# A decoder kernel: the first attention recorded in a fixed order, with the context attention's beginning beside its steps

## The chip, the cores and the metric

The kernel runs on 1 core of one Trainium2 chip. The metric is the device time of one execution in microseconds (us); the time before is 4245.74 us, the median of 3 runs (4244.13 to 4250.96). Five engines run side by side, each through its own queue in order: TensorE (PE) multiplies and transposes, VectorE (DVE) and ScalarE (ACT) work element by element, GpSimd (POOL) does a few additions, and SyncE (SP) issues the loads. An instruction waits on semaphores for the results that it needs, and whatever stands behind it in the same queue waits with it.

## The reference, cut to what matters

Two decoder layers work on `x` of 4 x 1024 x 256 in float32. Each layer has a self attention, a context attention and a feed-forward part. The change touches layer 0 only, up to the first steps of its context attention:

```python
def _L0_attn_ref(x, Wq, bq, Wk, bk, Wv, bv, Wo, bo):          # one head of 128
    Q = jnp.einsum('bsd,hd->bsh', x, Wq) + bq
    K = jnp.einsum('bsd,hd->bsh', x, Wk) + bk
    V = jnp.einsum('bsd,hd->bsh', x, Wv) + bv
    scores = jnp.where(causal, jnp.einsum('bqh,bkh->bqk', Q, K), -jnp.inf)
    attn = jax.nn.softmax(scores * jnp.float32(HEAD_DIM) ** (-0.5), axis=-1)
    return jnp.einsum('bsh,dh->bsd', jnp.einsum('bqk,bkh->bqh', attn, V), Wo) + bo

x = x + _L0_attn_ref(_layernorm(x), ...)
x = x + _L0_xattn_ref(_layernorm(x), ctx_1024, ...)           # 16 heads of 16, 77 context rows per batch
x = x + _L0_ffn_ref(_layernorm(x), ...)                       # ternary weights, 8 bit activations
x = x + _L1_attn_ref(_layernorm(x), ...); x = x + _L1_xattn_ref(...); x = x + _L1_ffn_ref(...)
return x
```

## The kernel before, in words

All of `x` stays in four SBUF tiles `X[b]` (128 rows x 8 tiles x 256), one for each batch; `load_x` issues their eight loads first of all. `B` is 4, `NTB` is 8 row tiles of 128 in a batch, `S` is 1024, `Z` is 77.

`l0_attn` (line 161) goes through the batches. For each it takes the row statistics of the eight tiles on DVE (lines 111 and 112), the root of the variance by a power on POOL (line 70), normalizes on DVE (line 118), adds the output bias to `X[b]` on POOL (`add_row`, line 156), turns the normalized tiles on PE (line 129) and copies the turned blocks alternately on DVE and ACT (`net.copy`, lines 141 and 143). Queries and keys are eight matmul passes of 512 columns each (line 191; a float32 matmul is two passes, so two halves by two parts by two passes), finished on ACT (line 194); the values are 32 passes of 128 columns (line 200), finished on DVE (line 204). Then each row tile `i` of the batch has eight stages:

1. scores on PE (line 214), only the `i + 1` blocks that the causal mask leaves
2. the mask on DVE (line 217), the row maximum `nm` (219) and its scaled copy `nb` (221)
3. the exponential on ACT with the row sum (line 224), and the sum's reciprocal on DVE (225)
4. `i + 1` transposes on PE (line 231)
5. their copies to `prT`, alternately on DVE and ACT (lines 141 and 143)
6. `i + 1` products with the values on PE (line 235)
7. a copy to `aT`, alternately on DVE and ACT
8. the projection on PE (line 240), added to `X[b]` on DVE (line 241).

No order is written out for this function: the framework's scheduler decides where each instruction stands in its engine's queue, and pools decide how far work may run ahead (two PSUM buffers for scores, two for transposes, two for outcomes).

When `l0_attn` has ended, its pools close, `Ffn` makes its tiles, and `l0_xattn` (line 247) begins: its weights are loaded into memory that the first attention has just left; `below`, the context keys `kb` (line 289 on PE, 294 on DVE) and values `v` (303 and 306) are made. From here on the order of PE, DVE and ACT is written out by hand (`manual_schedule`). `prologue(b)` is a generator of eight pieces which normalizes batch `b` again and makes the context attention's queries `qT`; `prologue(0)` runs through first. Then a loop over `u`, half a batch each, and four slots `s` in it: `maxima(u + 1, s)` (PE line 383, DVE 391 and 395; `turned` transposes the result at line 401 and copies it at 402), `weigh` of the slot before, `exponentials(u, s)` (PE lines 418 and 423, ACT 427), `outcome` (lines 447 to 467), and pieces of other work: one piece of `ahead` (the next batch's `prologue`) and three of `behind` (`ffn.weights`, which loads eight parts of the feed-forward weights, line 847, takes their absolute sums, line 858, and quantizes them, lines 812 to 814; later `ffn.rows`). The loop begins at `u = -1`, a round of four slots that has no exponentials yet:

```python
            ahead.append(prologue(0))
            while ahead:
                piece(ahead)
            neg = following = first = second = None
            ...
            for u in range(-1, U):
                if u % 2 and (u + 1) // 2 + 1 < B:
                    ahead.append(prologue((u + 1) // 2 + 1))
```

So `prologue(1)` runs beside the rounds -1 and 0, and the weights beside the rounds -1, 0 and 1. The feed-forward part, layer 1's attention (which takes most of the time, line 1312 above all) and the rest follow in the same order in both kernels.

Of the kernel before, what the change touches and what calls it, by code (L numbers as in the profile page):

```python
# [10 lines left out]
F32 = mybir.dt.float32  # L11
# [8 lines left out]
P = 128  # L20
B, S, D = 4, 1024, 256
Z = 77
NTB = S // P
# [6 lines left out]
class Net:  # L30
# [14 lines left out]
    def load_x(self):  # L45
        x = self.ins["x"].rearrange("(b t p) d -> b p t d", b=B, p=P)
        for b in range(B):
            for h in range(2):
                ts = slice(h * NTB // 2, (h + 1) * NTB // 2)
                self.nc.sync.dma_start(self.X[b][:, ts, :], x[b][:, ts, :])  # L50
# [110 lines left out]
def l0_attn(net):  # L161

    tc, nc = net.tc, net.nc
    with ExitStack() as ctx:
        w = ctx.enter_context(tc.tile_pool(name="w1", bufs=1))
        p2 = ctx.enter_context(tc.tile_pool(name="p1_2", bufs=2))
        p3 = ctx.enter_context(tc.tile_pool(name="p1_3", bufs=3))
        ps_s = ctx.enter_context(tc.tile_pool(name="ps1_s", bufs=2, space=PSUM))
        ps_t = ctx.enter_context(tc.tile_pool(name="ps1_t", bufs=2, space=PSUM))
        ps_o = ctx.enter_context(tc.tile_pool(name="ps1_o", bufs=2, space=PSUM))  # L170
# [3 lines left out]
        wo = net.load(w, "L0_attn_WoT", [P, D])  # L174
        bq = net.load(w, "L0_attn_bq", [P, 1])
        bk = net.load(w, "L0_attn_bk", [P, 1])
        bv = net.load_row(w, "L0_attn_bv", P)
        bo = net.load_row(w, "L0_attn_bo", D)
        causal = net.load(w, "c_causal", [P, P])
        scale = float(np.float32(P) ** np.float32(-0.5))  # L180
        for b in range(B):
            xnT = net.normalized_t(b, p2, ps_t)
            net.add_row(b, bo)
            qT = p2.tile([P, S], F32, name="qT")
            kT = p2.tile([P, S], F32, name="kT")
            for wt, bias, dst in ((wq, bq, qT), (wk, bk, kT)):
                for n in range(2):
                    cols = bass.ts(n, 512)
                    po = ps_o.tile([P, 512], F32, name="po")
                    for c in range(2):  # L190
                        nc.tensor.matmul(
                            po, wt[:, c, :], xnT[:, c, cols], start=(c == 0), stop=(c == 1)
                        )
                    nc.scalar.activation(dst[:, cols], po, AF.Identity, bias=bias)
            v = p2.tile([P, NTB, P], F32, name="v")
            for g in range(2):
                po = ps_o.tile([P, 4, P], F32, name="po")
                for t in range(4):
                    for c in range(2):
                        nc.tensor.matmul(  # L200
                            po[:, t, :], xnT[:, c, bass.ts(4 * g + t, P)], wv[:, c, :],
# [3 lines left out]
                    v[:, 4 * g : 4 * g + 4, :], po, bv.unsqueeze(1).to_broadcast([P, 4, P]), ALU.add  # L205
                )
            aT = p2.tile([P, S], F32, name="aT")
            rinv = p2.tile([P, NTB], F32, name="rinv")
            for i in range(NTB):
                n = (i + 1) * P  # L210
                sc = ps_s.tile([P, S], F32, name="sc")
                for j in range(0, n, 512):
                    m = min(512, n - j)
                    nc.tensor.matmul(
                        sc[:, j : j + m], qT[:, bass.ts(i, P)], kT[:, j : j + m], start=True, stop=True
                    )
                nc.vector.tensor_tensor(sc[:, n - P : n], sc[:, n - P : n], causal, ALU.add)
                nm = p3.tile([P, 1], F32, name="nm")
                nc.vector.tensor_reduce(nm, sc[:, :n], AX.X, ALU.max, negate=True)
                nb = p3.tile([P, 1], F32, name="nb")  # L220
                nc.vector.tensor_scalar(nb, nm, scale, None, ALU.mult)
                pr = p3.tile([P, S], F32, name="pr")
                sm = p3.tile([P, 1], F32, name="sm")
                nc.scalar.activation(pr[:, :n], sc[:, :n], AF.Exp, bias=nb, scale=scale, accum_out=sm)
                nc.vector.reciprocal(rinv[:, i : i + 1], sm)
# [2384 lines left out]
```

## Time and profile before

| what | value |
|---|---|
| median of 3 runs | 4245.74 us (4244.13 to 4250.96) |
| the profiled execution: its own time, its span | 4258.2 us, 4256.2 us |
| busy over the whole span | PE 93%, DVE 70%, ACT 38%, POOL 24% |
| granted PE clock, mean | 0.971 |
| first product on PE | at 10.8 us |
| last addition of the first attention (line 241) | at 191.4 us |
| first product of the context attention (line 289) | at 202.3 us |
| round -1 of the context attention's loop | 220.6 to 240.4 us |
| round 0 | 240.4 to 276.0 us |
| last exponentials of round 7 (line 427) | begin at 495.7 us |

In an answer by stretches, each line has the stretch, its length, then the busy time of PE, of PE's weight loads (PEld), DVE, ACT and POOL with the number of instructions, the granted PE clock (1.00 is full speed), the share of the DMA engines and the GB/s. In a timeline, each line has start, duration, engine, line of the code, operation, output<-input, and in brackets the idle time of the engine just before and what ended it. The profiled execution took 12.5 us more than the median, so a difference worked out in it is carried over to the median as it stands.

### The profile page before, as it was taken

Reading aid. Unit: us, or ns where it says so; the run is one execution under the profiler, and the core shown is the slowest. Engines: PE = TensorE matmul, PEld = TensorE weight load, DVE = VectorE, ACT = ScalarE, POOL = GpSimd, SP = SyncE. Lnnn points to the kernel's source line nnn. Section 1 sums busy time; section 2 is a strip of 40 time slices with the busy share of each in tenths; the row PEclk is TensorE's granted clock in tenths of the full one; section 3 lists DMA queues with packets and bytes.
Section 4 is the critical chain, followed back from the end, with each engine's and each line's share of the span. In section 5 each row is a group of like instructions: output and inputs, shape, how many; then the busy total and the mean of one; then the engine's idle time right before and its main releaser. Section 6 shows DMA issues by size and latency. Waiting matters only on the chain.

```text
span 4256.2 us, 58168 instructions
## 1 busy us (share of the span) xinstructions
PE 3957.2 (93%) x22392; PEld 2840.0 (67%) x22392; DVE 2992.6 (70%) x5484; ACT 1605.6 (38%) x2557; POOL 1026.4 (24%) x1218
## 2 busy tenths in 40 slices
PE   7889758999999999999999999997889899899999
PEld 5544324888788887888878877784555555557765
DVE  6555687889778987789878888776667567543224
ACT  2234445344333343333433333332555454212220
POOL 2000000334333433333333333331000000012215
PEclk9989979999999999999999999998999999899999
DMA  1010000000000000000000000000000000301213
GB/s 48 25 35 1 1 22 2 1 1 1 1 1 1 1 1 1 1 1 1 1 1 1 1 1 1 1 1 27 1 1 1 1 1 11 113 23 61 64 42 108
DMA packets 50911, 64.37 MB, mean 15 GB/s; under 512 B 8557, under 2 KB 44769, under 8 KB 50625
## 3 DMA queue, kind: packets, MB, share of 16 engines
q1 hardware_dynamic: 44145, 42.81, 3.2%
q0 software_dynamic: 6480, 17.70, 1.5%
q8 instruction: 185, 3.03, 0.3%
q14 instruction: 101, 0.83, 0.1%
HBM read 42.80 MB, written 17.69 MB: 14 GB/s over the span
## 4 chain that ended last, share of the span: by engine, by line
PE 67%; DVE 15%; ACT 2%; issue 1%; another core or an unknown queue 0%; DMA 0%; DVEq 0%; ACTq 0%; SPq 0%
PE sc L1312 35%; PE po L1341 5%; PE ph L2364 4%; PE ph L2292 3%; PE sc L1800 3%; DVE nm L1813 3%; DVE mx L1320 2%; DVE pr L1330 2%; PE po L1882 2%; PE po L2394 2%; PE po L2279 2%; PE pt L1748 1%; DVE prT L1851 1%; DVE km L1302 1%; PE pt L1850 1%
## 5 line engine op out<-in xcount | busy, mean ns | idle before, releaser
L1312 PE MATMUL sc<-qT,km 128*128 128x256 f32 x8064 | 1794.7, 382 | 9.0 <-DVE pr L1330 9.0
L1312 PEld LDWEIGHTS sc<-qT,km 128*128 128x128 f32 x8064 | 1521.8, 190 | 275.1 <-issue 62.4
L1333 ACT ACTIVATE pr<-pr,zb 128x1024 f32<-128x1024 f32 x512 | 588.2, 1149 | 1327.9 <-DVE pr L1330 1308.0
L1322 POOL PARTITION_ALL_REDUCE top<-mx x512 | 545.8, 1066 | 1466.1 <-DVE mx L1320 1466.1
L1320 DVE TENSOR_REDUCE mx<-sc 128x256 f32<-128x1024 f32 x512 | 625.2, 1221 | 323.1 <-PE sc L1312 321.6
L1330 DVE TENSOR_TENSOR pr<-sc,top 128x1024 f32<-128x1024 f32 x512 | 621.0, 1213 | 0.0
L1302 DVE SCALAR_TENSOR_TENSOR km<-kT,w_L_attn_conv_w,km 128x512 f32<-128x512 f32 x504 | 380.5, 758 | 24.7 <-ACT km L1289 20.0
L1325 POOL COPY tops<-top 32x256 f32<-32x256 f32 x512 | 269.6, 526 | 32.5
L1341 PE MATMUL po<-pr,v 128*32 128x256 f32 x4096 | 249.2, 384 | 0.0
L1813 DVE TENSOR_REDUCE nm<-sc 128x1 f32<-128x1024 f32 x128 | 156.1, 1220 | 79.4 <-PE sc L1800 79.3
L1827 ACT ACTIVATE pr<-sc,nb,rq 128x1024 f32<-128x1024 f32 x128 | 155.1, 1212 | 129.3 <-PE pt L1857 110.1
L1341 PEld LDWEIGHTS po<-pr,v 128*32 128x32 f32 x4096 | 120.4, 110 | 109.6 <-issue 43.2
L2364 PE MATMUL ph<-wgu,xnT 128*128 x568 | 180.4, 460 | 2.2 <-issue 1.6
L1289 ACT ACTIVATE km<-kT,w_L_attn_conv_w 128x512 f32<-128x512 f32 x252 | 173.5, 707 | 5.3 <-PE po L1095 5.3
L1850 PE MATMUL pt<-ident,pr 128*128 128x128 f32 x1024 | 142.7, 280 | 21.9 <-DVE X L1901 12.3
L2371 DVE TENSOR_TENSOR xnT<-ph,xnT 128x352 f32<-128x352 f32 x71 | 37.2, 524 | 171.0 <-ACT xnT L2370 133.8
L1865 POOL COPY rb<-rinv 128x256 f32<-128x256 f32 x32 | 12.9, 402 | 592.0 <-DVE rinv L1841 314.6
L1850 PEld LDWEIGHTS pt<-ident,pr 128*128 128x128 f32 x1024 | 111.4, 142 | 47.0 <-issue 18.8
L2364 PEld LDWEIGHTS ph<-wgu,xnT 128*128 128x128 f32 x568 | 102.3, 190 | 49.0 <-issue 3.0
L1800 PE MATMUL sc<-kT,qT 64*128 64x512 f32 x512 | 133.1, 624 | 0.2 <-ACT pr L1827 0.2
L1882 PE MATMUL po<-prT,v 128*64 128x256 f32 x1024 | 133.1, 392 | 0.2 <-DVE oT L1889 0.2
L1851 ACT COPY prT<-pt 128x512 f32<-128x512 f32 x128 | 68.9, 589 | 142.5 <-PE pt L1850 142.5
(515 smaller groups left out, 4871.7 us busy)
## 6 DMA issues: line engine op xcount, KB each, us to landing
yrows<-xnT SPq DMA_DIRECT2D x71, 128.0 KB, 1.7
X<-in_x SPq DMA_DIRECT2D x8, 512.0 KB, 8.0
out<-X SPq DMA_DIRECT2D x8, 512.0 KB, 2.8
wgu<-in_L_ffn_w_gate SPq DMA_DIRECT2D x8, 352.0 KB, 6.7
wgu<-in_L_ffn_w_up SPq DMA_DIRECT2D x8, 352.0 KB
raw<-in_L_ffn_w1T SPq DMA_DIRECT2D x4, 512.0 KB
raw<-in_L_ffn_w2T SPq DMA_DIRECT2D x4, 512.0 KB, 3.7
xrows<-xn SPq DMA_DIRECT2D x2, 1024.0 KB
```

The lines of the kernel that those rows point to most:

```text
L1302: nc.vector.scalar_tensor_tensor(km, keys, weight, km, ALU.mult, ALU.add)
L1312: nc.tensor.matmul(sc[:, j, :], km[:, c, bass.ts(j, P)], qT[:, c, bass.ts(i, Q2)], start=(c == 0), stop=(c == 1),)
L1320: nc.vector.tensor_reduce(mx, sc.rearrange("p j q -> p q j"), AX.X, ALU.max)
L1322: nc.gpsimd.partition_all_reduce(top, mx, P, bass_isa.ReduceOp.max)
L1325: nc.gpsimd.tensor_copy(tops[n][rows, i % (NQ, 2)[n], :], top[rows])
L1330: nc.vector.tensor_tensor(pr, sc, top.unsqueeze(1).to_broadcast([P, KT, Q2]), ALU.subtract)
L1333: nc.scalar.activation(pr, pr, AF.Exp, bias=zb[:, h : h + 1])
L1341: nc.tensor.matmul(po[32 * e : 32 * e + 32, :], v[:, n * KT + j, 4 * g + e, :], prs[e][:, j, :], start=(j == 0), stop=(j == KT - 1),)
L1800: nc.tensor.matmul(sc[e][:, bass.ts(n, 512)], lhsT[at], kT[at, d, bass.ts(n, 512)], start=True, stop=True,)
L1813: nc.vector.tensor_reduce(nm, sc[e], AX.X, ALU.max, negate=True)
L1850: nc.tensor.transpose(pt[:, n, :], pr[e][:, bass.ts(j + n, P)], net.ident)
L2364: nc.tensor.matmul(ph[:, k, :F], s["xT"][:, c, :], wgu[:, bass.ds(s["e"] * GU + (2 * c + k) * F, F)], start=(c == 0), stop=(c == 1),)
```

## The change

- `l0_attn` becomes a generator that shares the context attention's PSUM pools, and its order on PE, DVE and ACT is written out by hand. One step handles one row tile, 32 steps in all. A step records, in this order: the scores of its tile, the transposes (and copies) of the tile two steps behind, the mask and maximum of its own, the projection of the tile four steps behind, planned work, the exponential of its own, work handed in by the context attention (`beside`), and the products with the values of the tile two steps behind.
- The planned work of batch b + 1 stands in the eight steps of batch b: normalizing in the steps 0 to 3, and turning, queries, keys and values in the steps 4 to 7, three units each. The statistics of batch b + 2 stand in the steps 4 to 7 (`measure`). Batch 1 is an exception: its statistics stand in steps 1 to 3 and all of its normalizing in step 3. Batch 0 prepares its first half ahead of step 0, and the rest in steps 0 to 3.
- Normalizing goes from DVE to ACT (half of batch 0's stays). The power on POOL becomes twelve small DVE operations and one for the offset. All copies of turned tiles go to ACT; of the turned probabilities, the first four blocks go to DVE and the others to ACT; the copy to `aT` goes to ACT. The values are finished in pairs of tiles, and the bias is added on POOL in halves (1024 instead of 2048 columns).
- Row tiles go from the largest to the smallest in batches 1 to 3, and in the order 0, 1, 2, 3, 7, 6, 5, 4 in batch 0.
- The context attention's weights are loaded into memory of their own, behind the first attention's weights and the other batches of `x`. `context_keys` stands in steps 8 and 9, `context_values` in 10 to 13, `prologue(0)` and `prologue(1)` piece by piece in steps 16 to 30, and the four `maxima(0, k)` in steps 32 to 35, where only the tail of the first attention is left. Round -1 goes, and the loop begins at `u = 0`. `Ffn`'s tiles and the pool of its weights (`p2`) are made only when the first attention has ended, so the pieces of `ffn.weights` stand beside the rounds 0, 1 and 2.
- After that, the order of the instructions is that of the kernel before. The number of matmuls is the same.

```diff
-def l0_attn(net):
+def l0_attn(net, ps_s, ps_t, beside):
...
+        net.load_x(range(1, B))
+        yield
...
-        for b in range(B):
-            xnT = net.normalized_t(b, p2, ps_t)
-            net.add_row(b, bo)
...
+            def of(self, first, n):                       # class Statistics
+                for t in range(first, first + n):
+                    nc.vector.bn_stats(self.st[:, t, :], net.X[self.b][:, t, :])
+                    nc.vector.bn_aggr(self.mv[:, t, :], self.st[:, t, :])
+
+            def root(self, first, n):
+                ts = slice(first, first + n)
+                nc.vector.tensor_scalar(self.var[:, ts], self.mv[:, ts, 1], LN_EPS, None, ALU.add)
+                r = net.rsqrt(p2, self.var[:, ts], P, n, f"x{first}_{n}")
+                nc.vector.scalar_tensor_tensor(
+                    self.off[:, ts], self.mv[:, ts, 0], -1.0, r, ALU.mult, ALU.mult
+                )
...
+            def normal(self, st, first, n, shared=False):  # class Batch
+                for t in range(first, first + n):
+                    x, r = net.X[self.b][:, t, :], st.r[t]
+                    if shared and t % 2:
+                        nc.vector.tensor_scalar(
+                            self.xn[:, t, :], x, st.mv[:, t, 0:1], r, ALU.subtract, ALU.mult
+                        )
+                    else:
+                        nc.scalar.activation(
+                            self.xn[:, t, :], x, AF.Identity, bias=st.off[:, t : t + 1], scale=r
+                        )
+
+            def biased(self, h):
+                x = net.X[self.b][:, h * HT : (h + 1) * HT, :]
+                nc.gpsimd.tensor_tensor(
+                    x, x, bo.unsqueeze(1).to_broadcast([P, HT, D]), ALU.add
+                )
...
+        def prepare(bt, st, step):
+
+            if bt.b == 1:
+                measure(st, [step + k for k in range(1, 4)])
+                for h in range(2):
+                    plan(step + 3, lambda h=h: bt.normal(st, h * HT, HT), lambda h=h: bt.biased(h))
+            else:
+                for k in range(4):
+                    plan(step + k, lambda k=k: bt.normal(st, 2 * k, 2))
+                    if k % 2:
+                        plan(step + k, lambda k=k: bt.biased(k // 2))
+            for k, do in enumerate((
+                (bt.turn, 0), (bt.turn, 1), (bt.turn, 2),
+                (bt.turn, 3), (bt.query, 0), (bt.key, 0),
+                (bt.query, 1), (bt.key, 1), (bt.value, 0),
+                (bt.value, 1), (bt.value, 2), (bt.value, 3),
+            )):
+                plan(step + 4 + k // 3, lambda do=do: do[0](do[1]))
...
+        while True:
+            b, k = divmod(step, NTB)
+            if b < B:
+                if k == 0:
+                    now = bt
+                    if b < B - 1:
+                        bt = Batch(b + 1)
+                        prepare(bt, stats.pop(b + 1), step)
+                    if b < B - 2:
+                        stats[b + 2] = Statistics(b + 2)
+                        measure(stats[b + 2], [step + k for k in range(4, 8)])
+                i = (k if k < HT else 3 * HT - 1 - k) if b == 0 else NTB - 1 - k
+                tiles.append(Tile(now, i))
+                tiles[step].scores()
+            if 2 <= step < B * NTB + 2:
+                tiles[step - 2].turned()
+            if b < B:
+                tiles[step].maxima()
+            if 4 <= step < B * NTB + 4:
+                tiles[step - 4].project()
+            for do in at.pop(step, []):
+                do()
+            if b < B:
+                tiles[step].exponentials()
+            more = beside(step)
+            if 2 <= step < B * NTB + 2:
+                tiles[step - 2].weigh()
...
-            ahead.append(prologue(0))
+            ahead += [prologue(0), prologue(1)]
+            for c in range(2):
+                with_step(NTB + c, context_keys, c)
+            for b in range(B):
+                with_step(NTB + 2 + b, context_values, b)
+            for k in range(16):
+                with_step(2 * NTB + k, piece, ahead)
+            for k in range(4):
+                with_step(B * NTB + k, lambda k: turns.append(maxima(0, k, following)), k)
+                with_step(B * NTB + 1 + k, lambda: turns.pop(0)())
+            for _ in before:
+                pass
             while ahead:
                 piece(ahead)
+            p2 = ctx.enter_context(tc.tile_pool(name="p2_2", bufs=2))
+            ffn = new_ffn()
+            behind = [ffn.weights(p2, ps_t)]
...
-            for u in range(-1, U):
+            for u in range(U):
```

## The prediction

> **What bounds the kernel now.** I read the slices of the page first. PE is the fullest engine, but not at the beginning, and its clock drops there too:
>
> ```profile
> PE   7889758999999999999999999997889899899999
> PEclk9989979999999999999999999998999999899999
> ```
>
> A slice is 106 us, so the change plays in the first two and a half. I cut these into stretches (columns as in the section before):
>
> ```profile
> 0.00:10.81 10.81, 0.00 (x1) 0.00 (x1) 5.17 (x25) 1.28 (x1) 2.38 (x7) 1.00 0.85 283
> 10.81:26.50 15.69, 14.91 (x63) 10.03 (x64) 13.97 (x37) 3.92 (x6) 6.37 (x3) 1.00 0.39 123
> 26.50:38.50 12.00, 1.00 (x8) 0.60 (x6) 12.00 (x44) 0.50 (x3) 8.41 (x3) 0.68 0.00 0
> 38.50:66.90 28.40, 26.36 (x142) 19.26 (x143) 17.87 (x44) 9.10 (x23) 3.66 (x2) 0.90 0.01 1
> 66.90:108.20 41.30, 37.95 (x217) 27.43 (x216) 22.91 (x62) 13.79 (x32) 4.51 (x1) 1.00 0.00 1
> ...
> 191.40:202.25 10.85, 0.00 (x0) 0.00 (x1) 7.95 (x35) 0.00 (x0) 2.10 (x3) 0.64 0.56 171
> 202.25:220.60 18.35, 17.57 (x56) 10.12 (x56) 6.76 (x15) 3.12 (x5) 4.52 (x1) 0.84 0.15 41
> 220.60:240.40 19.80, 7.40 (x73) 5.15 (x72) 17.32 (x47) 1.75 (x5) 0.00 (x0) 0.62 0.17 54
> ```
>
> Three holes stand out: 12 us in which the scheduler let DVE do later batches' normalizing first, 10.9 us until the context attention's weights have landed, and round -1, where DVE is full and PE waits. The waits name them:
>
> ```profile
> ACT pr L224 <- DVE nb L221: 47.6, 20, 14.0
> PEld pt L231 <- ACT pr L224: 24.3, 15, 11.4
> PE pt L401 <- DVE tops L395: 12.4, 4, 3.9
> PE pt L289 <- DMA w_c_sel<-in_c_sel: 10.9, 1, 10.9
> ```
>
> **The work of PE that is left.** In the timeline eight passes of 512 columns begin 3.43 us apart from the next group: 0.43 each; 32 passes of 128 take 3.46, 0.107 each; 256 columns then take 0.215. A batch has 180 passes of 128 for scores, transposes and products (72 + 36 + 72: 19.3 us), 32 for values (3.4), 16 turns (1.7), 16 passes of 512 (6.9), 16 of 256 for the projection (3.4): 34.7 us, where the kernel takes 41.3 to 41.8. Four batches: 139. Context keys and values (8 passes of 308, 16 of 256): 5.5. Two prologues of 16 turns and 16 passes of 512: 17.2. Four `maxima` of 0.93: 3.7. Together 165.4 us up to round 0, which now begins at 240.4.
>
> **What PE will wait for, by walking through the steps.** On DVE I use 0.69 us for a copy of 512 columns (0.42 for 256, 0.28 for 128), 0.30 for the mask, 1.22 down to 0.28 for a maximum, 0.14 for `nb`, 0.48 for the projection's addition, 0.15 for a reciprocal, 0.42 for the values of two tiles, 0.53 for the statistics of a tile (the spacing at 192 us), 2.4 for the twelve root operations (196.3 to 198.8) and 0.2 for the offset, 0.36 for a normalized tile; on ACT 0.52 for a normalized tile (2.07 for four).
>
> - Lead-in. The first half of `X[0]` is there at 4.75. Four statistics (2.1) and a root (2.6) end at 9.5, so PE begins at about 10.3, as before. Turns, queries and keys of half a batch run at the slow pace of before's first passes (0.86 for 512), and ACT finishes the keys: scores at 17.3, with 4.3 us of work done. Lost: 13.0.
> - Steps 3 to 5. Batch 1's root ends at about 30.6; eight normalized tiles on ACT stand ahead of step 3's exponential, whose buffer the scores of step 5 want. PE is there at 32.5 and goes on at 36. Lost: 3.5.
> - Products behind the copy of `prT`: in steps without planned PE work only the projection (0.43) covers 0.69 and the handover, 0.3 us in some twelve steps: 3.5.
> - POOL's additions. Beside one of them DVE's normalizing stood still, as these two groups of eight show:
>
> ```profile
> 19.31 6.86 DVE L118 TENSOR_SCALAR xn<-X,mv_x,rstd_x 128x256 f32<-128x256 f32 x8 [1.30 <-POOL rstd_x L70]
> ...
> 70.07 2.67 DVE L118 TENSOR_SCALAR xn<-X,mv_x,rstd_x 128x256 f32<-128x256 f32 x8 [0.28 <-PE pt L129]
> ```
>
>   The difference is 4.2 us for an addition of 4.5. The bias now comes in eight halves of some 2.25 us (estimate, half of 4.5) between `nb`s, and twice whole. Ends: nothing, or 8 x 2.25 + 2 x 4.5 = 27. Most of it falls on DVE's slack; I take 2.
> - Steps 15 to 20, where DVE becomes the bound. Step 15: 1.9 for the tile, 1.3 for values, 1.1 for statistics, 2.6 for the root: 6.9, PE 4.2. Step 16: 2.7 and four statistics (2.1), PE 2.8. Step 17: 2.4 and 2.1, PE 2.3. Step 18: 2.7, a root, two normalized tiles: 5.8, PE 4.3. DVE 22.0 against 13.6, as each product waits for a copy queued behind all that. In 19 and 20 the prologue's turns wait for tiles normalized behind the same queue. The walk gives 33.6 us for 22.6 of PE. Lost: 11.
> - Steps 23 to 31, the same for `prologue(1)`, with little PE work beside it since no batch follows: waits of 0.4, 2.2, 5.8 (step 26, its turn), 2.7 and 2.7. Lost: 14.
> - Steps 32 to the start of round 0: masks and maxima of the context attention (3.6, then three times 1.5 on DVE) in series with PE, some 15 us for 6.2 of PE. Lost: 8.8.
>
> Sum: 165.4 + 13.0 + 3.5 + 3.5 + 2 + 11 + 14 + 8.8 = 221.2. Round 0 begins 19.2 us earlier.
>
> The Trainium skill ("SBUF — State Buffer", Who interferes with whom) says that DVE in a two-port mode and GpSimd exclude each other for whole instructions; every half bias would then cost its full 2.25 wherever DVE is the bound, which is in steps 15 to 19 (two of them) and 28: some 7 instead of 2. It also says ("TensorE: Matmul & The Clock Gate", Part 1) that an idle window of about 3.4 us halves the clock, and a busy one restores it; that speaks against the long wait of step 26 and the tail, and would add about 2 us for each. Neither figure is in the sum.
>
> **What else moves.** Loads: the other three batches of `x` now stand behind nine small loads on SP, which took 7.5 us to issue (7.6 to 15.1). `X[1]` is then issued at 10 and, by the page's 8.0 us to landing, there at 18, when step 1's statistics want it: 0 to 2 us of DVE, nothing in the sum. The context attention's weights follow, long before step 8; `raw` and the two feed-forward rows stay behind the first attention's end. The first sum stands one slot (about 8 us) behind its load, and one that was free took 3.7 to land, so I cost it at nothing; if its memory came free late, DVE would stop there for at most a landing, 4 us. ACT takes 28 normalized tiles (14.6 us), eight turned copies and eight copies to `aT` more, beside the 61 us that it worked in 240; apart from steps 3 to 5 that is hidden. Round 0 loses `prologue(1)`'s 8 us of PE, but its slots are bound by a chain (maxima, DVE, exponentials on PE, ACT 1.93): the four took 9.95, 8.57, 7.89 and 9.17. I keep the first, which ran at a low clock, and give 7.9 to the others: 33.6 for 35.6, gain 2. Three quantizations (2.15 each on DVE) move into round 2, whose DVE was busy 11.1 of 32: cost 1. Total: 19.2 + 2 - 1 = 20.2. The profiled execution would go from 4258.2 to 4238; carried over to the median 4245.7, that is 4225.
>
> **Rivals.**
> 1. The walk is too strict, and PE stays the bound through steps 15 to 31 as the copies are ready early. Then 20 of the 25 us there go, and 5 elsewhere: about 4200. For it: only PE's order and two buffers of scores force the meeting. Against: each product stands behind a copy in DVE's queue.
> 2. Slower: the fixed order ends each step in a handover (product waits for copy, copy behind the last step's maximum and addition). If that costs 1.2 us in each of 32 steps instead of the 3.5 us above, it adds 35: 4260. It decides from 1.0 us a step ((20.2 + 3.5 + 8.5) / 32). For it: before, the last tile, in series, took 8 us from its scores (182.5) to its projection (190.6). Against: two tiles of distance, where DVE has 2.5 to 3 us of 3.5 to 5.
> 3. It does not do what it says: the holes close, but PE's clock falls in the new ones. The rows grant 0.62 to 0.68 around holes. At 0.65 the 62 us of PE work in steps 15 to 20 and 23 to 31 take 33 more; the 25 of waits cover about half of it: 16 more, 4241, no change.
>
> **How the numbers follow.** About 0.2% (8.5 us) is what can be told from no change. My forecast gets 0.75, rival 1 0.10 (both faster), rival 3 0.09 (the same), rival 2 0.06 (slower). Range: down by 15 for the DVE waits and 7 for products and lead-in, up by 5 for POOL, 4 for the load and 8 for the clock: 4203 to 4242, which leaves out half of rivals 1 and 3 and all of 2.
>
> **What would show it.** Right: the 12 us and 10.9 us holes gone, scores from about 17 us, batches of 37 to 40 us, small PE waits on DVE in steps 15 to 20 and 24 to 28 with the root and normalizing in front, first exponentials of round 0 at about 223 us, and later stages shifted as a whole. Wrong: waits of PE on copies in every step; a clock below 0.9 from 60 to 200 us; DVE waiting for `raw` in round 0; or a change behind 300 us.

## The result, and the profile after

The changed kernel takes 4219.28 us (median of 4 runs, 4217.14 to 4222.46), the kernel before in the same comparison 4247.82. The ratio is 0.9937, with a 95% interval from 0.9924 to 0.9950: 28.5 us less. The forecast was 20.2 us less, or 4225.

Lines of the code have moved: L323 scores, L352 transposes, L357 and L359 the copies to `prT` on DVE and ACT, L365 products with the values, L368 the copy to `aT`, L374 projection, L231 normalizing on ACT, L246 turns, L256 queries and keys, L129 and L534 the prologues' turns and queries, L480 context keys, L573 the products of `maxima`, L585 its maximum, L591 its transpose. The profiled execution took 4222.46 us, its span 4220.7. The slices of the page, PE and its clock:

```profile
PE   8899568999999999999999999997989899899999
PEclk9989889999999999999999999998999999899999
```

PE's first slice rises from 7 to 8 and its third from 8 to 9; the fifth and sixth, 7 and 5 before, are 5 and 6, since what follows comes earlier. Behind them one digit of PE differs. The same in stretches (columns as before), cut at the scores of steps 0, 8, 16, 21 and 23, at the end of step 31's products and at round 0:

```profile
19.82:65.67 45.85, 42.43 (x219) 29.86 (x220) 27.19 (x93) 20.14 (x45) 7.01 (x3) 0.93 0.14 33
65.67:109.27 43.60, 43.60 (x262) 33.82 (x261) 28.40 (x89) 19.42 (x46) 4.71 (x2) 1.00 0.00 1
109.27:134.85 25.58, 20.26 (x123) 14.80 (x121) 23.60 (x85) 13.03 (x30) 4.72 (x2) 1.00 0.00 1
...
152.29:197.12 44.83, 40.90 (x227) 29.12 (x226) 29.49 (x95) 15.19 (x39) 4.54 (x1) 1.00 0.00 1
197.12:213.25 16.13, 11.24 (x87) 7.10 (x85) 10.77 (x22) 1.87 (x8) 0.00 (x0) 0.66 0.10 34
213.25:246.89 33.64, 28.12 (x189) 12.62 (x189) 8.27 (x10) 9.34 (x15) 0.00 (x0) 0.81 0.10 32
```

The two holes of 12 and 10.9 us are gone. Subtract the busy time of PE from the length: PE has no idle time in steps 8 to 15, 5.3 us in steps 16 to 20 (where DVE is busy for 23.6 of 25.6), 3.9 in steps 23 to 31, and 4.9 in the tail, where its clock is low too. Round 0 begins at 213.25 instead of 240.40, 27.2 us earlier. The first scores of layer 1's last attention stage (L1800 before, L2008 after) stand at 2956.9 instead of 2986.1, 29.2 earlier; layer 1's first scores (L1312, L1520) came 26.5 earlier (722.0 for 748.5). Round 0 itself took 2.0 less. So the change lies before and in round 0, within a wobble of some 3 us that later stages add between any two of these executions. (The spans differ by 35.5. The other 6 lie in the feed-forward products at the end of layer 1, L2500, which took 577.9 us from first to last in some profiled executions and 582.1 in others, whatever the edit, and 584.0 in that of before.)

The waits of PE up to round 0, each with total, count and longest:

```profile
PE pt L246 <- ACT xn L231: 12.7, 5, 10.3
PE pt L365 <- DVE prT L357: 7.2, 7, 1.7
PE pt L591 <- DVE rinv L369: 2.7, 1, 2.7
PE pt L591 <- DVE tops L585: 2.1, 2, 1.7
PE pt L129 <- DVE xn L118: 1.7, 1, 1.7
```

The first is the lead-in (10.3) and steps 3 to 5; the second is DVE in steps 16 to 18, 24 to 26 and 31; the third and fourth lie in the tail; the last is the wait of step 26, for which the forecast had 5.8. The lead-in and steps 3 to 5 in the timeline of PE:

```profile
12.90 3.78 PE L256 MATMUL pt<-xnT,w_L_attn_WqT 128*128 128x512 f32 x4 [0.68 <-ACT xnT L249]
...
19.82 0.49 PE L323 MATMUL sc<-kT,qT 128*128 128x128 f32 x2 [0.78 <-ACT kT L260]
...
35.76 0.33 PE L246 MATMUL pt<-ident,xn 128*128 128x128 f32 x1 [1.97 <-ACT xn L231]
...
40.02 1.65 PE L365 MATMUL pt<-prT,v 128*128 128x128 f32 x6 [0.96 <-ACT aT L368]
41.47 3.19 PE L323 MATMUL sc<-kT,qT 128*128 128x512 f32 x4
```

Such a group of four passes of 512 columns takes 3.78 and 3.19 us here, and 1.88 where the same line stands at 46.12: PE ran at half clock, in the second case from 38.3 to 45.2. And steps 16 and 17, where each product waits for a copy on DVE, which stands behind statistics and the root in step 16 and behind four statistics in step 17:

```profile
113.38 0.71 PE L365 MATMUL pt<-prT,v 128*128 128x128 f32 x4 [1.57 <-DVE prT L357]
...
117.78 0.49 PE L365 MATMUL pt<-prT,v 128*128 128x128 f32 x2 [1.65 <-DVE prT L357]
```

### The profile page after: what moved, and what is told of

Same layout as the page of the kernel before. It is cut to its first block, busy times and chain, and to the rows that moved or that the text cites. A ratio compares the mean times of both kernels' runs of the same rounds, so it can differ in the third digit from the quotient of the medians.

```text
span 4220.7 us, 58215 instructions
## 1 busy us (share of the span) xinstructions
PE 3950.9 (94%) x22392; PEld 2841.7 (67%) x22392; DVE 2984.2 (71%) x5514; ACT 1622.8 (38%) x2601; POOL 1019.4 (24%) x1218
## 4 chain that ended last, share of the span: by engine, by line
PE 67%; DVE 15%; ACT 1%; issue 1%; DMA 0%; SPq 0%; DVEq 0%; ACTq 0%
PE sc L1520 35%; PE po L1549 5%; PE ph L2572 4%; PE ph L2500 3%; PE sc L2008 3%; DVE mx L1528 3%; DVE pr L1538 3%; DVE nm L2021 3%; PE po L2090 2%; PE po L2602 2%; PE po L2487 2%; PE pt L1956 2%; DVE prT L2059 1%; DVE km L1510 1%; PE pt L2058 1%
## 5 line engine op out<-in xcount | busy, mean ns | idle before, releaser
L1520 PE MATMUL sc<-qT,km 128*128 128x256 f32 x8064 | 1793.1, 381 | 8.8 <-DVE pr L1538 8.8
L1520 PEld LDWEIGHTS sc<-qT,km 128*128 128x128 f32 x8064 | 1521.4, 190 | 273.7 <-issue 61.4
L2058 PEld LDWEIGHTS pt<-ident,pr 128*128 128x128 f32 x1024 | 111.6, 142 | 47.3 <-issue 18.8
L2008 PE MATMUL sc<-kT,qT 64*128 64x512 f32 x512 | 130.8, 615 | 0.3 <-ACT pr L2035 0.3
```

The costliest lines, as they stand in the source:

```text
L1520: nc.tensor.matmul(sc[:, j, :], km[:, c, bass.ts(j, P)], qT[:, c, bass.ts(i, Q2)], start=(c == 0), stop=(c == 1),)
L2008: nc.tensor.matmul(sc[e][:, bass.ts(n, 512)], lhsT[at], kT[at, d, bass.ts(n, 512)], start=True, stop=True,)
L2058: nc.tensor.transpose(pt[:, n, :], pr[e][:, bass.ts(j + n, P)], net.ident)
```

## The experiments

The experiments take parts of the change away, or change one suspected cost. The place to compare is the beginning of round 0, since all kernels have the same work up to there. Times are set against the kernel before on the same chip; in the last four rows these chips were slower throughout, so only the difference is to be read.

| kernel | median us | before there | difference | ratio, 95% interval | round 0 at |
|---|---|---|---|---|---|
| before | | | | | 240.40 |
| after | 4219.28 | 4247.82 | -28.5 | 0.9924 to 0.9950 | 213.25 |
| context attention's beginning behind | 4235.55 | 4249.11 | -13.6 | 0.9954 to 0.9979 | 224.08 |
| before, with early loads | 4244.42 | 4249.11 | -4.7 | 0.9978 to 0.9998 | 235.18 |
| projection three behind | 4227.14 | 4249.11 | -22.0 | 0.9928 to 0.9961 | 215.08 |
| batch 1 normalized by two engines | 4222.42 | 4249.11 | -26.7 | 0.9922 to 0.9955 | 211.06 |
| prologues' pieces earlier | 4217.55 | 4249.07 | -31.5 | 0.9913 to 0.9946 | 210.75 |
| PE kept busy at the start | 4218.02 | 4249.07 | -31.0 | 0.9914 to 0.9947 | 208.23 |
| late statistics | 4239.12 | 4249.07 | -10.0 | 0.9966 to 0.9985 | 229.47 |
| rising tiles | 4216.81 | 4249.07 | -32.3 | 0.9909 to 0.9943 | 211.90 |
| after, again | 4234.72 | 4261.67 | -27.0 | 0.9919 to 0.9946 | 212.09 |
| maxima early | 4222.13 | 4261.67 | -39.5 | 0.9887 to 0.9917 | 205.35 |
| three edits | 4232.63 | 4261.67 | -29.0 | 0.9920 to 0.9947 | 207.78 |
| three edits and maxima early | 4223.07 | 4263.71 | -40.6 | 0.9898 to 0.9925 | 204.77 |

**What the work beside the steps is worth.** Nothing is handed in; the same instructions follow when the first attention has ended:

```diff
-        before = l0_attn(net, ps_s, ps_t, lambda step: [do() for do in work.pop(step, [])])
+        before = l0_attn(net, ps_s, ps_t, lambda step: [])
...
             for _ in before:
                 pass
+            for step in sorted(work):
+                for do in work[step]:
+                    do()
```

> The first attention in its fixed order, but with nothing of the context attention beside it: keys, values, both prologues and the four maxima are recorded in one go after the last step. My theory (the order closes the 12 us hole and the waits inside the batches; the work beside it closes the other two holes): the attention's last projection by about 172 us, and then some 43 us of work that is half DVE and half PE, so that round 0 begins at 214 to 220 us instead of 213.3, and the time is 4220 to 4226. Rival 1 (what stands beside the steps brings most of the gain): round 0 at 230 us or later, 4236 or more. Rival 2 (the work beside costs as much as it hides, by DVE waits in steps 15 to 31): round 0 at 210 us or earlier.

Measured: 13.6 us of the 28.5 are left, and round 0 begins 10.8 later, between the theory (214 to 220) and rival 1 (230 or later). The timeline of PE behind the first attention:

```profile
173.71 2.24 PE L480 MATMUL pt<-w_ctxT,w_L_xattn_w_kv 128*128 128x308 f32 x8
...
187.11 1.99 PE L129 MATMUL pt<-ident,xn 128*128 128x128 f32 x8 [7.71 <-DVE xn L118]
```

The first attention alone is over by 173.7 on PE, where it took until 191.3 before. That comes from the written order and from the other division of the work among the engines together; no run separates the two. What then follows takes 35.0 us up to the first `maxima` at 208.7, for 22.7 of PE work. In the changed kernel that `maxima` begins at 197.9, 24.2 after 173.7. So the work beside the steps costs about its own 22.7 of PE time. What it saves is waits and, behind them, clock (0.90 granted in the 35.0 us): the 7.7 us for statistics, root and normalizing are the largest piece. Round 0 also took longer here (36.0 to its end, for 33.6).

**What the loads alone are worth.** The kernel before, with the context attention's weights loaded into memory of their own ahead of the first attention, and no other edit; the line below issues them, and the pools of PSUM follow later as before:

```diff
         causal = net.load(w, "c_causal", [P, P])
+        next(then)
```

> The kernel before, with one part of the change alone: the context attention's weights are loaded into memory of their own behind the first attention's weights. My theory: the 10.9 us hole at 191 us shrinks to what DVE needs for the first prologue's statistics, and round -1 begins 8 to 10 us earlier; time 4238 to 4240. Rival: the hole is not the loads' but DVE's (statistics, root and normalizing end at 200 us anyway), and PE's keys and values only move into it: 4 to 6 us, 4242 to 4244. Second rival: the loads were hidden, no change.

Measured: 4.7 us less than before, round 0 5.2 earlier, as the first rival said. PE no longer waits 10.9 us for `c_sel`, but behind the context keys and values another wait has grown, while DVE normalizes for the prologue:

```profile
203.13 1.94 PE L129 MATMUL pt<-ident,xn 128*128 128x128 f32 x8 [5.20 <-issue]
```

Half of a removed wait is taken over by the next chain.

**What the projection's distance is worth.**

```diff
-            if 4 <= step < B * NTB + 4:
-                tiles[step - 4].project()
+            if 3 <= step < B * NTB + 3:
+                tiles[step - 3].project()
```

> The changed kernel with the projection three tiles behind instead of four. My theory: by then the copy to aT has been ready for about a microsecond in nearly every step, so round 0 begins within 1.5 us of 213.3 and the time does not change. Rival: the copy stands behind the exponential of the step before on ACT, PE waits about 0.5 us for it in each of 32 steps, and round 0 begins 10 to 16 us later (4230 to 4235).

Measured: round 0 1.8 later and 2.7 longer, 6.5 us less gain; the intervals overlap, so the time alone would not show it. Neither the theory (within 1.5) nor the rival (10 to 16) came true. The longer round 0 is not shown to be the edit's: the same round takes between 31.6 and 36.3 us in these kernels. The wait up to there is in the trace. At distance three the projection wants a copy to `aT` that ACT makes behind eight normalized tiles:

```profile
40.03 1.22 PE L374 MATMUL pt<-w_L_attn_WoT,aT 128*128 128x256 f32 x2 [6.67 <-ACT aT L368]
```

That one wait holds most of it; the other eight together take 3.1. The fourth step of distance is worth something only where ACT's queue is long.

**Steps 3 to 5: is it ACT's eight tiles?** Batch 1's tiles are normalized alternately on DVE and ACT.

```diff
-                    plan(step + 3, lambda h=h: bt.normal(st, h * HT, HT), lambda h=h: bt.biased(h))
+                    plan(step + 3, lambda h=h: bt.normal(st, h * HT, HT, shared=True), lambda h=h: bt.biased(h))
```

> The changed kernel with batch 1's normalizing shared, four tiles on DVE and four on ACT, where all eight stood on ACT in step 3. My theory (the 9 us that PE loses between 33.8 and 45 us are ACT's eight tiles ahead of the exponential and of the turns, and the half clock that follows): the scores of step 5 begin about 3 us earlier (38.5 instead of 41.5), with the clock still low or not, round 0 at 208 to 210.5 us, time 4215 to 4217. Rival: what is late there is DVE's root (34.9 us), and DVE's four tiles only make it later: round 0 at 213 us or after.

Measured: from the scores of step 4 to those of step 6 it takes 16.5 us instead of 19.3, and the same four passes of step 5 are short:

```profile
39.19 1.92 PE L323 MATMUL sc<-kT,qT 128*128 128x512 f32 x4
```

This looked like the answer. But two later kernels that leave the normalizing on ACT alone took 16.8 there, with the clock full (prologues' pieces earlier; PE kept busy at the start), and five others took 18.8 to 19.2, with the clock halved (one of them, with rising tiles, has shorter tiles there). So the clock alone is worth 2.5. The shared normalizing is worth 1.5 where the clock is full in both: 15.3 in the kernel with three edits below, for 16.8. In the time nothing can be told (-26.7 against -28.5).

**Steps 15 to 31: is DVE the bound?**

```diff
-            for k in range(16):
-                with_step(2 * NTB + k, piece, ahead)
+            for step in (12, 13, 16, 17, 18, 19, 20, 21, 22, 23, 24, 25, 26, 27, 28, 29):
+                with_step(step, piece, ahead)
```

> The sixteen pieces of the two prologues move from steps 16 to 31 to steps 12, 13 and 16 to 29. In the changed kernel round 0 began at 213.25 us, and PE lost about 7 us in steps 15 to 20 and 6 in steps 23 to 31. Theory (DVE is the bound where pieces and the next batch's statistics meet): with two pieces in steps whose PE never waited, and none in the last two, round 0 begins at 208 to 211 and the kernel takes 2 to 5 us less than the changed one. Rival (PE is the bound throughout, so its work is only moved): round 0 at 213 within 1 us and no difference in time. Against both: if steps 12 and 13 are no freer than the others, new waits of PE on the copies of prT appear at 85 to 95 us and round 0 is later by up to 3 us.

Measured: round 0 at 210.75 and 3.0 us less, as the theory said, but not for its reason: 2.0 of the 2.5 us were there already at step 8 (63.71 for 65.67), ahead of the first moved piece, from the clock in steps 3 to 5. From step 16 to step 31's scores it took 85.9 us, for 85.7. The waits of PE up to round 0 changed names:

```profile
PE pt L129 <- DVE xn L118: 4.4, 2, 3.9
...
PE pt L365 <- DVE prT L357: 2.5, 4, 1.6
```

The waits for the copies fell by 4.7, those for normalized tiles rose by 2.7. The longest of these has another engine in it:

```profile
115.55 2.35 POOL L237 TENSOR_TENSOR X<-X,r_L_attn_bo 128x1024 f32<-128x1024 f32 x1 [30.77 <-DVE rt_x L93]
115.73 2.64 DVE L118 TENSOR_SCALAR xn<-X,mv_x,ri_x 128x256 f32<-128x256 f32 x2
...
118.11 1.22 PE L129 MATMUL pt<-ident,xn 128*128 128x128 f32 x4 [3.93 <-DVE xn L118]
```

Two normalized tiles take 0.73 on DVE where POOL is idle (at 126.51 in the changed kernel). Moved to this place they meet POOL's addition and take 2.64, PE waits 3.93 for them, and from 118 to 120 its granted clock is 0.50. So the edit bought a new wait with the old ones. It decides neither for the theory nor for the rival: PE still stands idle for 7.8 of the 85.9 us, so it is not bound by its own work alone.

**The first passes.**

```diff
+        pt = ps_t.tile([P, 512], F32, name="pt")
+        for k in range(44):
+            nc.tensor.transpose(pt[:, bass.ts(k % 4, P)], net.ident, net.ident)
         bt, st = Batch(0), Statistics(0)
```

> 44 transposes of the identity, whose result nobody reads, are put ahead of PE's first turn, so that PE is busy while the first half of x lands and is normalized. In the changed kernel the passes of the first queries and keys took twice the time of later ones (the first scores at 19.82 us instead of the 17.3 forecast). Theory (PE's clock is what is slow there): these passes take 0.43 us instead of 0.86, the first scores begin at 17 to 17.5 and everything behind moves by 2 to 2.5 us. Rival (DVE and ACT, which normalize and copy, set the start): the passes become shorter but the first scores begin within 0.5 us of 19.8, and the time stays.

Measured in the timeline of PE:

```profile
12.84 1.98 PE L256 MATMUL pt<-xnT,w_L_attn_WqT 128*128 128x512 f32 x4 [0.73 <-ACT xnT L249]
...
17.32 0.49 PE L323 MATMUL sc<-kT,qT 128*128 128x128 f32 x2 [0.78 <-ACT kT L260]
```

The first four passes take 1.98 instead of 3.78, the first scores come at 17.32 instead of 19.82, and all of it is kept. Steps 3 to 5 went without the low clock as well, and round 0 begins 5.0 earlier, as does layer 1's last attention stage (2952.0 for 2956.9). The theory is right for the start: the three kernels with these transposes have their first scores at 17.12 to 17.32, the nine without them at 18.77 to 20.37. The 2.5 us more in steps 3 to 5 are not shown to be the edit's, since the kernel with the earlier pieces, which is unchanged up to there, has them too. The time fell by 2.5 more than that of the changed kernel, inside the intervals.

**The statistics two batches ahead.**

```diff
-            if bt.b == 1:
+            if True:
...
                         stats[b + 2] = Statistics(b + 2)
-                        measure(stats[b + 2], [step + k for k in range(4, 8)])
```

> The statistics of batches 2 and 3 are no longer taken two batches ahead but in the batch just before, as batch 1's are in the changed kernel; order and everything else stay. Theory (the root and the normalizing then stand in one stretch, as in steps 3 to 5, where PE lost 9 us): 5 to 9 us more for each of the two batches, round 0 at 223 to 231, and 10 to 18 us more in time. Rival (steps 3 to 5 are dear because batch 0's first steps are short and x[1] lands late; the statistics are the same work wherever they stand): less than 2 us in round 0 and in time.

Measured: round 0 16.2 later, as the theory said, and 18.6 less gain, a little more than it said. PE's timeline in steps 12 and 20, where the next batch's turns stand:

```profile
88.33 0.70 PE L374 MATMUL pt<-w_L_attn_WoT,aT 128*128 128x256 f32 x2 [1.76 <-DVE v L495]
...
92.99 0.66 PE L246 MATMUL pt<-ident,xn 128*128 128x128 f32 x4 [1.75 <-ACT aT L368]
...
140.98 0.70 PE L374 MATMUL pt<-w_L_attn_WoT,aT 128*128 128x256 f32 x2 [3.18 <-DVE xnT L141]
```

Step 12 takes 10.8 us instead of 5.5, step 20 takes 12.9 instead of 5.2 (its end at half clock). DVE makes the root and the offset from 85.4 to 87.9; an addition for the values, a copy, a maximum and an addition follow behind it, and PE's projection and turns wait for each in turn. Of the single parts this is the dearest to take away. The kernel here also normalizes all eight tiles in one step, as batch 1 does, so the two share these 16 us.

**The order of the tiles.**

```diff
-                i = (k if k < HT else 3 * HT - 1 - k) if b == 0 else NTB - 1 - k
+                i = k
```

> All batches take their eight row tiles in rising order instead of the longest first. Theory (the last tile decides how long the attention drains: with 512 + 512 columns of products and eight transposes behind two copies of 0.69 us each it ends in series, and the tile after it covers nothing; the short tiles now meet the next batch's normalizing at the end of a batch): round 0 5 to 10 us later, 5 to 10 us more in time. Rival (each batch has the same work whatever the order): round 0 within 2 us of 213.25 and no difference.

Measured: round 0 1.4 earlier, the time 3.8 lower than the changed kernel's, inside the intervals. The theory falls: largest tiles first is worth nothing here that could be measured. The end of the attention lies beside the four `maxima` whichever tile is last, which may be why; no run shows that.

**The tail.** Three runs on one chip, and a fourth on another:

> The changed kernel once more, beside the next two. Theory: 26 to 31 us less than the kernel before; its first rows show whether PE runs at half clock from about 38 to 45 us in steps 3 to 5 again (step 6's scores at 50.4 us) or, as in two of the other runs, does not (48.5 or earlier): if that is chance, it may be either here with the same code.

> The four maxima of the context attention's round -1 stand beside steps 28 to 31 instead of 32 to 35. In the changed kernel the 16.1 us from step 31's products to round 0 held 6.2 us of PE work. Theory (the tail is a series of PE, maximum and turn, 3.4 us for each of the four; beside steps that PE fills it costs only its 0.9 us each): round 0 begins 6 to 9 us earlier, at 204 to 207, and the time falls by 5 to 9 us. Rival (the maxima take both buffers of scores, so that the next step's scores wait for DVE's two maxima and its mask): each of steps 28 to 31 takes 2 to 3 us longer, and round 0 moves by less than 2 us.

```diff
             for k in range(4):
-                with_step(B * NTB + k, lambda k: turns.append(maxima(0, k, following)), k)
-                with_step(B * NTB + 1 + k, lambda: turns.pop(0)())
+                with_step(B * NTB - 4 + k, lambda k: turns.append(maxima(0, k, following)), k)
+                with_step(B * NTB - 3 + k, lambda: turns.pop(0)())
```

The changed kernel repeated its gain (-27.0), again with half clock in steps 3 to 5 (18.9 from step 4 to step 6). With the maxima beside steps 28 to 31, round 0 begins 6.7 earlier and the time is 12.6 lower; the intervals of the two ratios do not overlap. PE in steps 28 to 31:

```profile
184.66 0.88 PE L323 MATMUL sc<-kT,qT 128*128 128x384 f32 x2 [0.53 <-DVE tops L585]
...
200.05 0.79 PE L573 MATMUL sc<-kb,qT 32*128 32x154 f32 x12 [0.92 <-ACT pr L340]
```

The buffers of scores cost what these brackets show, 1.5 us in all, as the products and the prologue's queries stand between. The clock is full from 197 to 212, where it was half from 201 to 214 in the kernel beside it, and round 0 took 31.6 us (to 236.99) for 33.4. That makes 8.5 up to round 1, the upper end of the theory's range; 7.2 of it are there at the first scores of layer 1 (709.8 for 717.0) and 4.6 at its last attention stage, and 4.6 more come in layer 1's last products (587.6 for 592.2), which vary by as much without an edit. So the trace supports 5 to 8.5 of the 12.6.

> Three edits together: the transposes that keep PE busy while x lands, batch 1's normalizing shared by DVE and ACT, and the prologues' pieces two steps earlier. Theory (the first removes half clock in the first passes, the second the wait behind ACT's eight tiles in steps 3 to 5, the third at most 0.5 us): scores from 17.3, step 6 at 44 to 45.5, round 0 at 206 to 208, and 4 to 7 us less than the changed kernel in the same runs. Rival (the three took their gains from the same chance, whether the clock halves in steps 3 to 5): no more than 3 us less.

The three edits bring the first scores to 17.29, step 6 to 43.92 and round 0 to 207.78, 4.3 earlier than the kernel beside them, and layer 1's last attention stage to 2941.4 (2952.0). The median is only 2.1 lower and the runs spread from 4224.94 to 4240.38, although the profiled execution is 8.3 shorter. Which of the two counts is open.

> The three edits of the run before with the maxima beside steps 28 to 31 as well. Theory (they act in different places: PE's first passes, steps 3 to 5, the tail): scores from 17.3 us, round 0 at 198 to 201, and 35 to 45 us less than the kernel before. Rival (moved two steps earlier, the prologues' pieces leave steps 30 and 31 without cover, so the maxima wait there for their buffers and the tail keeps its length): round 0 at 205 or later, no more than 40 us less, as with the maxima alone.

Added to the maxima they bring 0.6 at round 0 (204.77, next to the rival's 205 and far from the theory's 198 to 201) and 1.1 in the difference (40.6, just past the rival's 40). The rival's mechanism is there, but beside another. Of the 5.3 us that this kernel is ahead of the one with the maxima alone at step 6 (43.74 for 49.04) and still at step 16 (102.57 for 107.86), 1.7 are lost by step 24, in a stretch where the two normalized tiles again meet POOL's addition (PE waits 3.94), and 3.1 from there to step 31's scores. In that stretch and just behind it PE waits 1.6, 1.0 and 0.9 us in the `maxima` of steps 29 to 31 for the exponential whose buffer they want, as the rival said. In time the two kernels can't be told apart, so the best version found is the one with a single edit, the change with its four maxima four steps earlier: 39.5 us under the kernel before.

## Why the prediction was right, step by step

The sign, the place and the range were right; the median lies 5.7 us under the forecast, and the gain is 28.5 for 20.2. The sum put 55.8 us of losses on top of 165.4 of work; the trace has 213.25 - 165.4 = 47.9. A loss is, as in the forecast, the length of a stretch less its counted work.

| step of the sum | forecast | measured | how read |
|---|---|---|---|
| lead-in | 13.0 | 15.5 | 19.82 less 4.3 of work |
| steps 3 to 5 | 3.5 | 6.9 | PE idle 3.4, and 3.5 lost to half clock in 6.9 us |
| copies of `prT`, and POOL | 5.5 | 0 | no idle time from 65.67 to 109.27 |
| steps 15 to 20 | 11 | 7.3 | 29.9 from 104.94 to 134.85 for the walk's 22.6 of work; PE idle for 5.3 |
| steps 23 to 31 | 14 | 5.9 | 44.8 from 152.29 to 197.12 for 38.9 at the forecast's 0.107 a pass; PE idle for 3.9 |
| tail | 8.8 | 9.9 | 16.1 for 6.2 of work |
| not in the sum | 0 | 2.4 | the rest: passes a little slower than counted (17.4 for 17.3 in steps 21 and 22) |

That the total came so close is partly luck: three rows of the table were 17.3 too large and four 9.4 too small.

- **Lead-in.** The step used the slow pace but multiplied it wrongly: it left 7.0 us (10.3 to 17.3), but 4.3 us of work at half clock are 8.1 busy (10.28 to 19.82 less two waits of 0.7 and 0.8), which with the waits ends at 19.8. The kernel with PE kept busy has them at 17.32, so the difference is the clock's.
- **Steps 3 to 5.** The size of the wait was right (3.4 for 3.5), its working only in part. The eight tiles on ACT are the cause, but DVE's root ended at 34.9 and not at 30.6, and PE waited 2.5 for the tiles themselves, to turn them, and 1.0 for a copy behind the exponential; the scores of step 5 did not wait for a buffer. The clock behind it is not in the sum; rival 3 had it, for other steps.
- **Copies, POOL.** Mis-sized: in steps 8 to 15 the copy is there in time, without a handover.
- **DVE in steps 15 to 31.** This was the step that failed most: 25 forecast, 13.2 measured, of which PE stands idle for 9.2. (The rest is beside the waits: four products that were counted at 0.43 take 0.54 after one, 113.38 to 113.92 above.) The load on DVE was right: its work of steps 15 to 18 took 21.5 us (105.7 to 127.2) for 22.0. So were the waits for copies in steps 24 and 25: these steps lose 0.4 and 1.9, for 0.4 and 2.2. What was too dear are the waits of the prologues' turns: step 26 loses 2.6 for 5.8, the two waits of 2.7 behind it do not show (steps 27 and 28 lose 0.1 each), and steps 19 and 20 lose 1.3 together. PE waits for the one result that it needs and not for DVE's whole step. In step 18 that is the copy at the step's head (from 121.73; PE goes on at 122.55); the root and the first two normalized tiles behind it, until 127.2, run beside PE's products and next scores. Nor can DVE's queue get a whole step ahead, as each step begins with a copy of what PE turns in that step. The line of step 24 shows this, and the other, of PE, is step 26's wait:

```profile
162.20 0.42 DVE L357 COPY prT<-pt 128x256 f32<-128x256 f32 x1 [3.44 <-PE pt L352]
```

```profile
171.83 0.78 PE L129 MATMUL pt<-ident,xn 128*128 128x128 f32 x4 [1.66 <-DVE xn L118]
```

How the walk came to its 5.8 for step 26 is not written down, so that part stays open.

- **Round 0.** 33.6 forecast, 33.64 measured, which is luck to this digit: the slots took 10.1, 8.8, 7.4 and 7.4 for 9.95 and three times 7.9, and the same round takes 31.6 to 36.3 us in these kernels. The 1 us for the quantizations in round 2 can't be told within the wobble behind it (27.2 + 2.0 at round 1, 26.5 and 29.2 in layer 1).
- **The parts.** They do not add up: 16.2 (statistics and spread normalizing), 10.8 (work beside) and 1.8 (projection) are lost at round 0 when each is taken away from the whole, and 5.2 is won by the loads put alone into the kernel before.
- **The signs.** Holes gone, waits of PE on DVE and the shift as a whole: as forecast. Batches of 37 to 40 us: no, 43.6 in steps 8 to 15, without idle time of PE. First exponentials at about 223: they begin at 222.26, but by accident, 9.0 after the beginning of round 0; from the 221.2 of the sum that would have been 230.

Rival 1 (PE stays the bound) was half right: 12 of the 25 us went, where it had 20. Rival 2 would have shown as a wait in every step; steps 8 to 15 have none. Rival 3 named the right mechanism in the wrong place: from 45.2 to 202 the clock is full through all the DVE waits, and it falls in steps 3 to 5 and in the tail, for 7 us of half clock and some 20 around the tail's end.

The Trainium skill ("SBUF — State Buffer", Who interferes with whom) says that DVE in a two-port mode and GpSimd exclude each other. The trace agrees on the mechanism: a root operation of 0.17 us took 1.40 while POOL added the bias (the lines are below). In the changed kernel it costs PE no wait in the steps that the forecast named: of the additions at 117.51, 128.00 and 183.46 one slowed DVE (two normalized tiles at 129.47 took 1.36 instead of 0.73), and PE has no idle time from 128.05 to 162.60. The forecast's bound of 7 by that page was too high, and so were the 2 of the sum. That is the place's luck, though: in the kernel with the earlier pieces the same exclusion added 1.9 us to two tiles for which PE waited.

## What to carry to other kernels

Where a busy engine alternates with serial chains, put the chain's beginning beside the busy steps: the work still costs its own engine time, and what is saved is its waits and the low clock behind them. Price a wait by what stands ahead of the one result that is needed, and not by all that the other engine does in a step (13.2 us here, for 25). When you move work, look what a third engine does at the new place: here a removed wait came back as another. Where a short series is left at the end (four times product, maximum, turn), look whether its inputs were ready some steps earlier; here that one move was worth more than the three other edits together (6.7 for 4.3 us at round 0, in kernels measured side by side).

## What the runs showed of the hardware

In steps 3 to 5 of the changed kernel PE's clock fell from 1.00 to 0.50 without a long pause:

```profile
33.80:38.20 4.40, 1.98 (x9) 1.03 (x9) 4.09 (x16) 3.09 (x7) 0.94 (x1) 1.00 0.00 0
...
38.30:45.20 6.90, 5.94 (x17) 3.79 (x18) 0.41 (x3) 4.36 (x11) 3.62 (x2) 0.51 0.01 2
```

The Trainium skill ("TensorE: Matmul & The Clock Gate", Part 1: The HAM clock gate) names, in its table of the two states, an idle window of about 3.4 us. Here the longest wait was 1.97 us, with some passes between it and the next ones (PE busy for 1.98 of the 4.4 us ahead of the fall). The clock halved so in six of the eight kernels that leave batch 1's normalizing and the projection as they are, and not in the other two: one has the transposes at the start, the other has no edit ahead of step 12. The measurement decides: waits of less than 2 us, close together, were enough, though not every time. What decides is not shown. A wait of 1.66 in step 26, with PE busy around it, left the clock full.

In the first stretch the granted clock is recorded as full while the passes took twice their time (the 3.78 above, inside it); there only the durations tell:

```profile
10.28:19.82 9.54, 8.09 (x16) 3.92 (x16) 5.92 (x24) 2.94 (x6) 2.34 (x1) 1.00 1.06 376
```

And the operation of DVE that met POOL's addition (POOL 11.35 to 13.69, DVE 12.32 to 13.72), in the timelines of the two:

```profile
11.35 2.34 POOL L237 TENSOR_TENSOR X<-X,r_L_attn_bo 128x1024 f32<-128x1024 f32 x1 [7.79 <-DMA r_L_attn_bo<-in_L_attn_bo]
```

```profile
12.32 1.40 DVE L202 TENSOR_SCALAR var<-mv 128x4 f32<-128x4 f32 x1
```

The statistics just before it, at 11.67, kept their 0.39 us beside the same addition: the exclusion held for the one operation of DVE and not for the other.
